# PSUM as one pool of eight banks, expert columns by single banks, and two small jobs moved to GpSimd

## The chip, the cores and the metric

One core of one Trainium2 chip runs the whole program in one launch. The metric is the device time of one execution in microseconds (us). Five engines have queues of their own, each worked through in order: TensorE (PE in the profile, PEld for its weight loads), VectorE (DVE), ScalarE (ACT), GpSimd (POOL) and SyncE (SP), which starts most transfers; GpSimd starts the indirect transfers. TensorE writes its results into PSUM, which this program uses as eight banks of 128 partitions x 512 floats.

## The reference, cut to what matters

`x` is 16 batches of 512 tokens of 128 numbers, all in 32-bit floats. Two layers follow each other:

```
xn = layernorm(x)                                # (x - mean) / sqrt(var + 1e-5)
x  = x + linear_attention(xn) + moe(xn)
xn = layernorm(x)
x  = x + chunked_softmax_attention(xn) + channel_mix(xn)
```

- Linear attention: 16 heads of 8, rotary embedding, features elu + 1, causal sums over k v; the result is divided by its causal denominator and goes through `Wo`.
- moe: 8 experts of width 512, `square(relu(x w_fc)) w_proj`; each token takes the two with the highest router probability, with weights that sum to one. A shared expert of the same form sees every token.
- Chunked softmax attention: 16 heads of 8, chunks of 64 queries that see all keys up to their chunk's end, with a gate per row from two steps of a small dynamic, and an output projection.
- Channel mix: `sigmoid(xr W_r) * (square(relu(xk W_k)) W_v)`, with xr and xk mixed from a token and the one before it.

## The kernel before, in words

**Four chains and a planner.** Batches go in five groups (3, 4, 4, 3, 2). For each group there are four generators. `dispatch` does the first layernorm, the router, the top two and the slots, and sends every token's row to its two slots in memory by 128-row indirect transfers on GpSimd (`send`, L1095). `slot_tiles` reads the slots back in tiles of 128 rows of one expert and runs the experts. `layer0` does linear attention and the shared expert, `layer1` all of the second layer, which begins with `combine`: it fetches the experts' rows (`fetch`, L1114, indirect again). The generators do not issue instructions: each call on `V`, `S`, `G`, `M` or `SP` records an operation in a `Program`, in the order in which the chains are interleaved by planned times. `Program.run` (L332) then deals out the real order. It keeps a clock for each engine with estimated costs (`COSTS`, and `TURN` for TensorE when the form of a matmul's tile changes), takes among the operations that are ready on an engine the earliest recorded (VectorE operations that read PSUM go first, `_rank`), and emits it. So the order on each engine is fixed when the program is built. All instructions so emitted have the line of the helper, L261. A `unit` is a run of matmuls that is dealt out as one piece; without it, operations of other chains can come between any two matmuls. The indirect transfers are "spaced": at least 1900 ns of the planned clock apart, and each is made to wait for the last matmul emitted before it. The square root of the layernorm is given 2600 ns more than other operations of its size.

**PSUM.** Two pools, each with its own line of requests: `ps_big`, three slots of two banks, and `ps_one`, two slots of one bank (L509). A slot that comes free goes back into a heap by its time, and the earliest free one is taken (`_take`, L414). Pairs hold scores (`sc`, `st`), the outputs by heads, q and k of both layers, the shared expert's hidden columns (`h_ps`) and the experts' (`hg_ps`); single banks hold transposes, router logits, `y` and `yg_ps`.

**Around the change.**
- `layernorm_T` (L649): mean and variance on VectorE, `ln_rstd` by a Sqrt activation on ScalarE and a reciprocal on VectorE, then `xn` on VectorE and its transposes on TensorE. It runs 32 times.
- `linear_operands` (L831): eight transposes of the features `qr` into one pair of banks (`qkT_ps`); ScalarE copies q and k out (`q0T`, `k0T`), and makes from the same PSUM tile four masked copies of q (`q0m`, two tiles of two halves), each by a Copy activation whose scale is a column of the constant `pick`. The masked copies feed the matmuls `sc<-q0m,k0T`.
- `shared_expert` (L1010) and `hidden` (L1168): two matmul groups of 512 columns fill a pair of banks, and one Relu of 128x1024 empties it; a square on VectorE or GpSimd follows. `project` (L1184) accumulates two tiles of `yg_ps` in one bank, `projected` (L1298) computes q and k of the second layer.

Of the kernel before, what the change touches and what calls it, by code (L numbers as in the profile page):

```python
# [159 lines left out]
class Base:  # L160


    def __init__(self, slots, make):
        self.slots, self.make, self.tile = slots, make, None
        self.writers, self.readers = [], []
        self.left, self.free_at, self.users = 0, 0.0, []

    def made(self):
# [5 lines left out]
class Slots:  # L174
# [1 line left out]


    def __init__(self, n, ahead):
        self.free, self.asked, self.taken, self.waiting = [0.0] * n, [], 0, []
        self.ahead = ahead  # L180


class Pool:
# [6 lines left out]
    def tile(self, shape, dtype, tag, name, bufs=None):  # L190
        n = bufs or self.bufs
        slots = self.tags.setdefault(tag, Slots(n, self.ahead))
        kw = {"bufs": bufs} if bufs else {}
        base = Base(slots, lambda: self.pool.tile(shape, dtype, tag=tag, name=name, **kw))
        slots.asked.append(base)
        base.psum = self.psum
        base.turn = len(slots.asked) - 1
        return View(base, shape)


class Op:
# [25 lines left out]
class Program:  # L227
# [21 lines left out]
    def call(self, name, api, method, args, kw):  # L249
        views = [a for a in (*args, *kw.values()) if isinstance(a, View)]  # L250
        o = kw.get("out", args[0] if args else None)
        writes = [o.base] if isinstance(o, View) else []
        reads = [v.base for v in views if v is not o]
        n = math.prod(o.shape[1:]) if isinstance(o, View) else 0
        later = 0.0

        def made(a):
            return a.made() if isinstance(a, View) else a

        def emit():  # L260
            return getattr(api, method)(*map(made, args), **{k: made(a) for k, a in kw.items()})  # L261

        if name == "PE":
            later = 60.0
            form = (args[1].shape[0], o.shape[0])
            if method == "transpose":
                cost = 112.0
            elif args[1].shape[0] == 32:
                cost = max(0.425 * n, 56.0)
            elif o.shape[0] == 32:  # L270
                cost = max(0.425 * n, 56.0)
            else:
                cost = max(1.68 * n, 224.0)
        elif method == "dma_start":
            cost, later = 80.0, 512.0 * n
        else:
            form = method if (name, method) in COSTS else None
            if name == "DVE" and method in ("tensor_scalar", "tensor_scalar_min", "tensor_scalar_max"):
                form = "fast"
            if method in ("tensor_reduce", "bn_stats"):  # L280
                n = math.prod(args[1].shape[1:])
            least, each = COSTS[name, form]
            cost = least + each * n
            if kw.get("func", args[2] if len(args) > 2 else None) == AF.Sqrt:
                cost += 2600.0
        op = self.add(name, emit, reads, writes, cost, later)
        if name == "PE":
            (self.unit_of[0] if self.unit_of else op).form = form
        return op
# [42 lines left out]
    def run(self):  # L332
# [20 lines left out]
        while emitted < len(self.ops):  # L353
# [46 lines left out]
            for base in op.bases:  # L400
                base.left -= 1
                base.free_at = max(base.free_at, end + op.later)
                if not base.left:
                    heapq.heappush(base.slots.free, base.free_at + HANDOVER)
                    waiting, base.slots.waiting = base.slots.waiting, []
                    for other in waiting:
                        offer(other, 0.0)
# [6 lines left out]
    def _take(self, op, start, offer):  # L414
# [4 lines left out]
            by_slots.setdefault(id(b.slots), []).append(b)  # L419
        ready = start  # L420
        for bs in by_slots.values():
            slots = bs[0].slots
            if len(slots.free) < len(bs):
                slots.waiting.append(op)
                return False
            if any(slots.asked[slots.taken + k] is not b for k, b in enumerate(bs)):
                ahead = bs[-1].turn - slots.taken
                if ahead > slots.ahead or not self._passes(new):
                    (slots.waiting if ahead > slots.ahead else self.put_off).append(op)
                    return False  # L430
            ready = max(ready, heapq.nsmallest(len(bs), slots.free)[-1])
        if ready > start:
            offer(op, ready)
            return False
        for bs in by_slots.values():
            slots = bs[0].slots
            for b in bs:
                heapq.heappop(slots.free)
                b.has = True
                while slots.taken < len(slots.asked) and hasattr(slots.asked[slots.taken], "has"):  # L440
                    slots.taken += 1
# [5 lines left out]
    def _passes(self, new):  # L447
# [8 lines left out]
                    also.setdefault(id(b.slots), set()).add(b)  # L456
        for bs in also.values():
            slots = next(iter(bs)).slots
            if len(slots.free) < len(bs):
                return False  # L460
            if any(b not in bs for b in slots.asked[slots.taken : slots.taken + len(bs)]):
                return False
# [26 lines left out]
def two_layers(ctx: ExitStack, tc: tile.TileContext, x, small, const, w_fc, w_proj, out):  # L489
# [16 lines left out]
    p2 = pool("p2", 2)  # L506
    p3 = pool("p3", 3)
    tiny = pool("tiny", 2)
    ps_big = pool("ps_big", 3, 24, space=bass.MemoryType.PSUM)  # L509
    ps_one = pool("ps_one", 2, 24, space=bass.MemoryType.PSUM)  # L510

    def big(name):
        return ps_big.tile([P, 2, 512], F32, tag="big", name=name)

    def one(name):
        return ps_one.tile([P, 512], F32, tag="one", name=name)

    def follows(i, first):

# [81 lines left out]
    V.reciprocal(rda, rda)  # L601
    V.tensor_mul(rda, rda, alpha)
    program.lag = 0
    eps = fixed.tile([P, 1], F32, tag="eps", name="eps")
    V.memset(eps, LN_EPS)
    zeros = fixed.tile([P, 1, D], F32, tag="zeros", name="zeros")
    G.memset(zeros, 0.0)
    program.lag = 1000
# [40 lines left out]
    def layernorm_T(xs, xT, name, tag, bufs):  # L649
# [4 lines left out]
            V.bn_stats(st[:, t, :], xs[:, t, :])  # L654
            V.bn_aggr(mv[:, t, :], st[:, t, :])
        rstd = tiny.tile([P, NT], F32, tag="ln_rstd", name=f"ln_rstd_{name}")
        S.activation(rstd, mv[:, :, 1], AF.Sqrt, bias=eps, scale=1.0)
        V.reciprocal(rstd, rstd)
        xn = p2.tile([P, NT, D], F32, tag=tag, name=f"xn_{name}", bufs=bufs)
        for t in range(NT):  # L660
            V.tensor_scalar(
# [169 lines left out]
    def linear_operands(xnT, b, home):  # L831
# [62 lines left out]
            )  # L894
        yield

        pts = big(f"qkT_ps_{b}")
        for s in range(2):
            for t in range(NT):
                M.transpose(  # L900
                    pts[:, s, t * P : (t + 1) * P], qr[:, t, s * D : (s + 1) * D], ident
                )
        q_tag, k_tag, bufs = home["T"]
        qT = p2.tile([P, T], F32, tag=q_tag, name=f"q0T_{b}", bufs=bufs)
        S.copy(qT, pts[:, 0, :])
        kT = p2.tile([P, T], F32, tag=k_tag, name=f"k0T_{b}", bufs=bufs)
        S.copy(kT, pts[:, 1, :])
        qms = []
        for u in range(2):
            tag, bufs = home["q0m"]  # L910
# [2 lines left out]
            )  # L913
            for o in range(2):
                r = 2 * u + o
                S.activation(qm[:, o, :], pts[:, 0, :], AF.Copy, scale=c_("pick")[:, r : r + 1])
            qms.append(qm)
        yield
        return qT, kT, qms
# [1 line left out]
    def linear_attention(operands, b, home):  # L921
# [4 lines left out]
        def scores(t):  # L926
# [14 lines left out]
            for pr, sc in enumerate(scs):  # L941
                tag, bufs = home["am"]
                am = p2.tile([P, 2, 512], F32, tag=tag, name=f"am_{b}_{t}_{pr}", bufs=bufs)
                V.tensor_tensor(
                    am.rearrange("p j (t q) -> p (j t) q", q=P),
                    sc.rearrange("p j (t q) -> p (j t) q", q=P),
                    causal.unsqueeze(1).to_broadcast([P, 2 * NT, P]), ALU.mult,
                )
                ams.append(am)
            return ams  # L950
# [59 lines left out]
    def shared_expert(b, xnT, oT, home):  # L1010
# [3 lines left out]
            p2.tile([P, 2, T], F32, tag="hid", name=f"h_{b}_{fp}", bufs=4) for fp in range(2)  # L1014
        ]
        for fp in range(2):
            ph = big(f"h_ps_{b}_{fp}")
            for i in range(2):
                f = 2 * fp + i
                M.matmul(  # L1020
                    ph[:, i, :], wfc_s[:, f * P : (f + 1) * P], xnT, start=True, stop=True
                )
            hf = hs[fp]
            S.activation(hf, ph, AF.Relu)
            (V if fp or b < GROUPS[0] else G).tensor_tensor(hf, hf, hf, ALU.mult)
            yield
        yield
        py = one(f"y_{b}").rearrange("p (t d) -> p t d", d=D)
        for t in range(NT):
            cols = slice(t * P, (t + 1) * P)  # L1030
            M.matmul(py[:, t, :], oT[:, cols], w_("wo0"), start=True, stop=False)
            for f in range(NF):
                M.matmul(
                    py[:, t, :], hs[f // 2][:, f % 2, cols], wpj_s[:, f, :], start=False, stop=(f == NF - 1)
                )
        V.tensor_tensor(xs, py, xs, ALU.add)
        SP.dma_start(passed["x1", b], xs.rearrange("p t d -> p (t d)"))
        yield
# [87 lines left out]
    def slot_tiles(g):  # L1126
# [39 lines left out]
            return xgT  # L1166

        def hidden(xgT, ws, q, pair):  # L1168
            ph = big(f"hg_ps_{g}_{q}_{pair}")
            for ii, (wf, _) in enumerate(ws):  # L1170
                i = 2 * pair + ii
                for f in range(NF):
                    M.matmul(
                        ph[:, ii, f * P : (f + 1) * P], wf[:, f * P : (f + 1) * P],
                        xgT[:, i * P : (i + 1) * P], start=True, stop=True,
                    )
            h = p2.tile([P, 2, FF], F32, tag="hid", name=f"hg_{g}_{q}_{pair}", bufs=4)
            o = h[:, 0 : len(ws), :]
            S.activation(o, ph[:, 0 : len(ws), :], AF.Relu)

            (V if pair or g == 0 else G).tensor_tensor(o, o, o, ALU.mult)
            return h
# [1 line left out]
        def project(h, ws, n):  # L1184

            py = one(f"yg_ps_{g}_{n}")
            for ii, (_, wp) in enumerate(ws):
                for f in range(NF):
                    M.matmul(
                        py[:, ii * P : (ii + 1) * P], h[:, ii, f * P : (f + 1) * P],  # L1190
                        wp[:, f, :], start=(f == 0), stop=(f == NF - 1),
                    )

            y = p2.tile([P, 2, D], F32, tag="yg", name=f"yg_{g}_{n}")
            m = len(ws)
# [102 lines left out]
    def projected(xT, b):  # L1298

        ps = big(f"qk1_{b}")  # L1300
        for i in range(2):
            M.matmul(ps[:, i, :], wqk1[:, i, :], xT, start=True, stop=True)
        qk = p2.tile([P, 2, T], F32, tag="qk", name=f"qk_{b}", bufs=1)
        S.copy(qk, ps)
        return qk
# [403 lines left out]
```

## Time and profile before

| | |
|---|---|
| time, median of 3 runs | 1670.35 us (1669.26 to 1676.13) |
| the profiled execution | 1665.29 us |
| its span, first to last instruction | 1663.5 us |
| mean granted clock of TensorE | 0.973 |
| instructions in the trace | 36439 |
| transfers | 167.03 MB, mean 100 GB/s |

The span lies 1.8 us inside the profiled execution's time. A group of the profile reads: line, engine, operation, output from input with shapes, how often; then busy time and mean ns of one; then the idle time of the engine just before them and who ended it. A busy time is the union of an engine's records, so a mean is that union divided by the count or the mean of single records where they overlap.

### The profile page before, as it was taken

The numbers are of one execution on the slowest core, as the hardware profiler recorded it, in microseconds if no ns is written. First come the engines' busy times: TensorE is split into PE (matmuls) and PEld (weight loads), VectorE is DVE, ScalarE is ACT, GpSimd is POOL, SyncE is SP. The second block draws the span as 40 slices with busy tenths as digits, with TensorE's granted clock in tenths as the row PEclk, the third lists the DMA queues.
The fourth block names the chain that finished last, engine by engine and source line by source line (L and its number), as shares of the span: only waits on it lengthen the run. The fifth ranks groups of instructions, "written<-read, shape, count | busy, mean of one in ns | idle before, by whom it ended". The sixth has DMA issues, their size and how long they took to land.

```text
span 1663.5 us, 36439 instructions
## 1 busy us (share of the span) xinstructions
PE 1547.3 (93%) x14439; PEld 1021.8 (61%) x14439; DVE 1207.5 (73%) x2474; ACT 778.2 (47%) x1191; POOL 539.1 (32%) x485
## 2 busy tenths in 40 slices
PE   4889799999999999999999989999999999999996
PEld 3578776666766566566666656666565656565443
DVE  7875268877578874976758796968786858786773
ACT  4343334545445634444544655454545444535444
POOL 1415255075125421453033603242136202135020
PEclk8899999999999999999999999999999999999998
DMA  5367777144334423243322243324133313110000
GB/s 155 106 211 233 219 218 212 49 141 118 96 107 127 127 87 96 72 121 97 90 90 79 78 122 96 96 63 124 35 94 92 110 33 86 30 51 23 20 1 14
DMA packets 154986, 167.03 MB, mean 100 GB/s; under 512 B 13248, under 2 KB 100672, under 8 KB 154816
## 3 DMA queue, kind: packets, MB, share of 16 engines
q1 hardware_dynamic: 146624, 147.91, 29.9%
q0 software_dynamic: 8192, 16.79, 3.3%
q8 instruction: 114, 1.87, 0.5%
q14 instruction: 56, 0.46, 0.1%
HBM read 122.83 MB, written 41.81 MB: 99 GB/s over the span
## 4 chain that ended last, share of the span: by engine, by line
PE 53%; DVE 10%; issue 5%; ACT 3%; POOL 1%; DMA 0%; SPq 0%; POOLq 0%; ACTq 0%; DVEq 0%
PE o L261 10%; PE sc L261 10%; PE st L261 8%; PE yg_ps L261 5%; PE hg_ps L261 5%; DVE maxima L261 4%; PE y L261 3%; PE h_ps L261 2%; PE qkv L261 1%; PE qk L261 1%; PE ho_a L261 1%; ACT ex L261 1%; PE oh_a L261 1%; PE mx L261 1%; PE cm_r L261 1%
## 5 line engine op out<-in xcount | busy, mean ns | idle before, releaser
L261 DVE TENSOR_REDUCE maxima<-sc 128x2 f32<-128x768 f32 (+2 forms) x448 | 385.8, 912 | 84.6 <-PE sc L261 83.0
L261 ACT ACTIVATE ex<-st 128x1024 f32<-128x1024 f32 x320 | 313.1, 1025 | 177.5 <-PE st L261 176.3
L261 PE MATMUL st<-qa,ka 32*128 32x384 f32 (+3 forms) x2048 | 213.4, 471 | 9.6 <-DVE maxima L261 5.9
L261 PE MATMUL sc<-ka,qa 32*128 32x512 f32 (+2 forms) x1792 | 213.8, 511 | 3.7 <-DVE maxima L261 1.0
L1095 POOL DMA_INDIRECT rows<-xn,pl_slot x128 | 135.1, 1055 | 225.6 <-PE y L261 64.2
L261 PE MATMUL yg_ps<-wp,hg 128*128 128x128 f32 x1304 | 188.5, 287 | 17.5 <-DVE hg L261 9.4
L261 PEld LDWEIGHTS yg_ps<-wp,hg 128*128 128x128 f32 x1304 | 162.6, 195 | 66.9 <-issue 36.6
L1114 POOL DMA_INDIRECT back<-results,pl_slot x128 | 128.4, 1003 | 222.7 <-PE st L261 38.4
L261 PE MATMUL hg_ps<-xgT,wf 128*128 128x128 f32 x1304 | 182.5, 285 | 10.8 <-issue 6.3
L261 DVE TENSOR_TENSOR am<-sc,const_sb 128x1024 f32<-128x1024 f32 x128 | 151.3, 1218 | 53.7 <-PE sc L261 49.2
L261 PEld LDWEIGHTS hg_ps<-xgT,wf 128*128 128x128 f32 x1304 | 163.5, 196 | 35.9 <-issue 23.8
L261 PE MATMUL o<-ex,vpad 128*32 128x512 f32 (+3 forms) x2048 | 175.1, 447 | 1.7 <-ACT yg L261 1.3
L261 PEld LDWEIGHTS st<-qa,ka 32*128 32x128 f32 x2048 | 104.0, 186 | 81.4 <-issue 26.4
L261 ACT ACTIVATE hg<-hg_ps 128x1024 f32<-128x1024 f32 x84 | 84.2, 1002 | 135.7 <-PE hg_ps L261 135.3
L261 POOL TENSOR_TENSOR hg<-hg 128x1024 f32<-128x1024 f32 x34 | 64.6, 1901 | 224.1 <-ACT hg L261 223.9
L261 PEld LDWEIGHTS sc<-ka,qa 32*128 32x128 f32 x1792 | 90.5, 185 | 70.5 <-issue 25.8
L261 PEld LDWEIGHTS o<-ex,vpad 128*32 128x32 f32 x2048 | 52.2, 110 | 83.8 <-issue 59.5
L261 DVE TENSOR_TENSOR hg<-hg 128x1024 f32<-128x1024 f32 (+1 forms) x50 | 62.0, 1241 | 56.4 <-ACT hg L261 56.4
L261 ACT COPY oTs<-o 128x256 f32<-128x256 f32 (+1 forms) x96 | 42.7, 445 | 120.2 <-PE o L261 119.5
L261 ACT COPY yg<-yg_ps 128x256 f32<-128x256 f32 x84 | 30.9, 368 | 131.6 <-PE yg_ps L261 108.6
L261 PE MATMUL o<-am,vpad 128*32 128x128 f32 x2048 | 81.8, 281 | 8.7 <-DVE am L261 8.0
L261 PE MATMUL sc<-q0m,k0T 32*128 32x256 f32 x1024 | 81.3, 410 | 1.6 <-ACT ex L261 1.0
(193 smaller groups left out, 2289.1 us busy)
## 6 DMA issues: line engine op xcount, KB each, us to landing
wf<-in_w_fc SPq DMA_DIRECT2D x163, 256.0 KB
wp<-in_w_proj SPq DMA_DIRECT2D x163, 256.0 KB
results<-yg SPq DMA_DIRECT2D x79, 128.0 KB
xg<-rows SPq DMA_DIRECT2D x37, 256.0 KB
rows<-zeros SPq DMA_DIRECT2D x2, 2496.0 KB
x_in<-in_x SPq DMA_DIRECT2D x16, 256.0 KB
x<-x SPq DMA_DIRECT2D x16, 256.0 KB
out<-rr SPq DMA_DIRECT2D x16, 256.0 KB
```

Source lines behind the costliest of these rows:

```text
L261: return getattr(api, method)(*map(made, args), **{k: made(a) for k, a in kw.items()})
L1095: i = nc.gpsimd.indirect_dma_start(out=rows.made()[:, :], out_offset=bass.IndirectOffsetOnAxis(ap=slot.made(), axis=0), in_=row.made(), in ...
L1114: "POOL", lambda: nc.gpsimd.indirect_dma_start(out=o.made(), out_offset=None, in_=results.made()[:, :], in_offset=bass.IndirectOffsetOnAxi ...
```

## The change

Four things change.

1. PSUM becomes one tile of eight banks. `big` and `one` ask the same line of requests (`Banks`); the planner assigns one free bank, or two adjacent free ones, and picks the placement with the least of (time it is ready + 400 ns for each bank that leaves its neighbour free). Candidates are tried by number, and a later one must be strictly better.
2. The hidden columns of both kinds of expert, and q and k transposed, take single banks; each bank is emptied by its own Relu or copy. `y`, `hg`, `yg` and `qk1` matmuls become units.
3. `q0m` is made by GpSimd from the copied `q0T` in SBUF.
4. The inverse root is made by GpSimd: add 1e-5, then raise to -0.5. The planner's extra cost for a square root goes.

The mask of the causal scores (`am`) is written with a four-dimensional pattern instead of a three-dimensional one, since the two banks are now a slice of a larger tile.

```diff
+class Banks:
+    def __init__(self, pool, n, ahead):
+        self.pool, self.n, self.whole = pool, n, None
+        self.slots = Slots(n, ahead)
+        self.slots.free = [(0.0, k) for k in range(n)]
...
+    def place(slots, bs, start):
+        free = {k: max(t, start) for t, k in slots.free}
+        best = None
+        def alone(k, rest):
+            return (k ^ 1) in rest
+        def fit(i, rest, at, ready, odd):
+            nonlocal best
+            if i == len(bs):
+                if best is None or ready + 400.0 * odd < best[0][0] + 400.0 * best[0][1]:
+                    best = ((ready, odd), list(at))
+                return
+            for k in sorted(rest):
+                ks = range(k, k + bs[i].banks)
+                if all(j in rest for j in ks):
+                    left = {j: t for j, t in rest.items() if j not in ks}
+                    cost = sum(alone(j, left) for j in ks)
+                    fit(i + 1, left, at + [tuple(ks)], max([ready] + [rest[j] for j in ks]), odd + cost)
...
-            if kw.get("func", args[2] if len(args) > 2 else None) == AF.Sqrt:
-                cost += 2600.0
...
-    ps_big = pool("ps_big", 3, 24, space=bass.MemoryType.PSUM)
-    ps_one = pool("ps_one", 2, 24, space=bass.MemoryType.PSUM)
+    banks = Banks(
+        ctx.enter_context(tc.tile_pool(name="psum", bufs=1, space=bass.MemoryType.PSUM)), 8, 48
+    )
...
-        S.activation(rstd, mv[:, :, 1], AF.Sqrt, bias=eps, scale=1.0)
-        V.reciprocal(rstd, rstd)
+        G.tensor_scalar_add(rstd, mv[:, :, 1], LN_EPS)
+        G.tensor_tensor(rstd, rstd, root, ALU.pow)
...
-        pts = big(f"qkT_ps_{b}")
-        for s in range(2):
+        q_tag, k_tag, bufs = home["T"]
+        both = []
+        for s, (tag, n) in enumerate(((q_tag, "q0T"), (k_tag, "k0T"))):
+            pts = one(f"qkT_ps_{b}_{s}")
             for t in range(NT):
...
+            oT = p2.tile([P, T], F32, tag=tag, name=f"{n}_{b}", bufs=bufs)
+            S.copy(oT, pts)
+            both.append(oT)
...
-                S.activation(qm[:, o, :], pts[:, 0, :], AF.Copy, scale=c_("pick")[:, r : r + 1])
+                G.tensor_scalar_mul(qm[:, o, :], qT, c_("pick")[:, r : r + 1])
...
-            ph = big(f"h_ps_{b}_{fp}")
...
-            S.activation(hf, ph, AF.Relu)
+                ph = one(f"h_ps_{b}_{f}")
+                M.matmul(ph, wfc_s[:, f * P : (f + 1) * P], xnT, start=True, stop=True)
+                S.activation(hf[:, i, :], ph, AF.Relu)
...
         py = one(f"y_{b}").rearrange("p (t d) -> p t d", d=D)
-        for t in range(NT):
+        with program.unit():
+            for t in range(NT):
...
         def hidden(xgT, ws, q, pair):
-            ph = big(f"hg_ps_{g}_{q}_{pair}")
...
+                ph = one(f"hg_ps_{g}_{q}_{i}")
+                with program.unit():
+                    for f in range(NF):
...
+                S.activation(h[:, ii, :], ph, AF.Relu)
...
             py = one(f"yg_ps_{g}_{n}")
+            with program.unit():
...
     def projected(xT, b):
         ps = big(f"qk1_{b}")
+        with program.unit():
```

## The prediction

> **What bounds the kernel now.** I read the page's busy line, slices and chain first, then a table of windows by stage.
>
> ```profile
> PE 1547.3 (93%) x14439; PEld 1021.8 (61%) x14439; DVE 1207.5 (73%) x2474; ACT 778.2 (47%) x1191; POOL 539.1 (32%) x485
> ...
> PE   4889799999999999999999989999999999999996
> ...
> PE 53%; DVE 10%; issue 5%; ACT 3%; POOL 1%; DMA 0%; SPq 0%; POOLq 0%; ACTq 0%; DVEq 0%
> ```
>
> ```profile
> 0.00:50.00 50.00, 25.45 (x119) 16.04 (x123) 37.23 (x145) 21.13 (x40) 10.14 (x26) 0.82 0.43 132
> 50.00:100.00 50.00, 43.80 (x534) 33.03 (x524) 40.64 (x103) 21.90 (x45) 21.86 (x22) 0.97 0.40 126
> 100.00:300.00 200.00, 180.47 (x1539) 148.31 (x1535) 125.84 (x266) 77.66 (x123) 84.22 (x72) 0.95 0.72 221
> 300.00:1600.00 1300.00, 1249.66 (x11877) 801.39 (x11880) 967.38 (x1878) 633.66 (x953) 420.23 (x364) 0.99 0.29 84
> 1600.00:1664.00 64.00, 47.89 (x394) 23.00 (x388) 36.39 (x85) 23.82 (x31) 2.66 (x3) 0.86 0.03 9
> ```
>
> The columns are length, busy time of PE, PE's loads, DVE, ACT and POOL, granted clock, DMA share, GB/s. TensorE is the bound from 100 us on (96% between 300 and 1600); only the first 50 us belong to the start and the last 64 to one batch's dependent chain. So an edit pays if it takes something out of TensorE's own queue: a matmul, a change of tile form, or a wait. ACT's 778 and POOL's 539 us are no bound by their sums.
>
> But "busy" hides short waits. I took every matmul's end, less the end before it, less its own streaming time. Streaming alone sums to 1228 us. Leaving the 128x128 form costs 197 ns (409 times), leaving a 32-row form 216 (370), leaving a 32-column form 143 (236): 194 us. The start and end are 14 us. The other 227 us of the 1663.5 are waits, by what the program makes each matmul wait for: 1273 that wait for one other engine lose 115 ns each (146 us), 186 for two 209 (39), 166 for TensorE's own earlier writes and another engine 300 (50), 58 for its own alone 88 (5); those with no wait come out at -2 ns (-12). By the engine last waited for, the gross losses are 292 us (so 0.77 of each counts): DVE 141, ACT 87, transfers 32, TensorE 27, POOL 5.
>
> Next, the groups that the edit touches, from the list of groups kept apart by shape.
>
> ```profile
> L261 ACT ACTIVATE hg<-hg_ps 128x1024 f32<-128x1024 f32 x79 | 81.2, 1027 | 128.9 <-PE hg_ps L261 128.5
> ...
> L261 ACT ACT_TABLE_LOAD x48 | 61.6, 1283 | 21.2 <-PE st L261 19.2 <-PEq L1699 0.7 <-DVE phi L261 0.6
> ...
> L261 POOL TENSOR_SCALAR ka<-qk,const_sb 128x512 f32<-128x512 f32 x32 | 50.7, 1583 | 0.0
> ...
> L261 ACT ACTIVATE q0m<-qkT_ps,const_sb 128x512 f32<-128x512 f32 x64 | 39.4, 713 | 0.0
> ...
> L261 ACT ACTIVATE ln_rstd<-ln_mv,eps 128x4 f32<-128x4 f32 x32 | 9.6, 298 | 16.4 <-DVE ln_mv L261 16.1
> ...
> L261 ACT ACTIVATE hg<-hg_ps 128x512 f32<-128x512 f32 x5 | 3.0, 599 | 6.9 <-PE hg_ps L261 6.9
> ```
>
> **Forms: -8 us.** Counted in the two programs' orders, the streaming matmuls are the same 14439, but grouping (units around y, hg, yg and qk1) cuts changes of form: 382, 348 and 250 against 409, 370 and 236. At 197, 216 and 143 ns that is 186 against 194 us. Nothing hides it.
>
> **Bank pool and single columns: -7 us (-31 to +20).** In the new program no matmul waits on TensorE's own writes (224 before), 1364 wait for one engine and 277 for two. At the old means that is 157 + 58 - 13 = 202 against 227: -25. Against it stands how soon a bank is used again. Both orders use a bank again 2430 times, but ties go to the lowest number: bank 0 gets 395 turns and bank 7 210, where the six banks of pairs had about 310 each. I measured the slack (TensorE work between the last write and the next, less the eviction's duration): 131 places below nothing against 120, 262 below 300 ns against 202, 702 below 1 us against 583. Priced by the old mean wait of each class this is 159 against 148 us: +11. Leaving out the matmuls that waited on TensorE itself it is 118 against 148 less 31 saved, which is the lower bound -31; the upper, +20, takes the shortfalls alone (65 against 47 us, 53 measured). The classes overlap with the kinds, so I take the middle of -25 and +11.
>
> **ACT: -5 us (0 to -32).** Away go 47 of 48 table loads (47 x 1.283 = 60), 32 square roots (9.6) and 64 q0m copies (64 x 0.713 = 46); each split Relu gives back 2 x 0.599 - 1.027 = 0.171, so +13 for the 79 hg pairs and +6 for the 32 h pairs. Net some -96 of 778 us, 12%. If TensorE's waits on ACT (87 x 0.77 = 67) shrank likewise: -8. But loads stand where ACT has slack:
>
> ```profile
> 732.00 1.28 ACT L261 ACT_TABLE_LOAD   x1
> 733.29 0.30 ACT L261 ACTIVATE ln_rstd<-ln_mv,eps 128x4 f32<-128x4 f32 x1
> 733.50 0.56 ACT L261 COPY oTs<-o 128x512 f32<-128x512 f32 x1
> 734.08 1.28 ACT L261 ACT_TABLE_LOAD   x1
> ```
>
> In the 228 us from 0.5 before to 3.5 after a load TensorE lost 0.181 us per us, elsewhere 0.176, so the loads cost it about 1. The far end, -32, would take away all 41 us lost in those windows. I take -5, since earlier Relu halves also release matmuls sooner. A rule that would enlarge this: the Trainium skill, "ScalarE: Activation LUTs", What ACT_TABLE_LOAD costs, adds a drain of some 1380 ns to the 1283 of the load; by it the 47 would be worth about 125 us of ACT, an estimate. The rows above leave no gap before or after the load, so here it is 1.28.
>
> **q0m on POOL: +6 us (+4 to +16).** The four halves move behind the q0T copy (0.59): ACT needed 2.4 us for its four in batch 0 (they overlap a little); POOL needs 4 x 1.58 = 6.3, by the ka row, the same operation and shape. Total 7 us, plus about 1 us for each indirect DMA interleaved (L1095, 0.96 each; up to five in batches 0, 1, 3, 4). The distance in TensorE's work from the transposes to the second q0m tile is 3.6, 6.5, 6.1, 8.3, 8.6, 9.5 us in batches 0 to 5, 6.3 to 6.9 in 6, 11 and 12, and over 14 in the rest, which hide it. The shortfalls sum to 19 us against 3 to 9 before; most of it (12) falls in batches 0 and 1, where TensorE has holes anyway. Behind a waiting q0m on POOL stand the spaced indirect DMAs of dispatch, and then the experts' gathers.
>
> **The start: +3 us (-3 to +24).** The first inverse root now needs POOL before xn, the first transposes and all that follows. Between POOL's memsets and this operation the new program puts a reload of POOL's operations. Before, the same reload stood ahead of the first hg square, inside a stretch in which POOL idled:
>
> ```profile
> 183.81 0.96 POOL L1095 DMA_INDIRECT rows<-xn,pl_slot  x1 [0.48 <-PE yg_ps L261]
> 212.71 1.89 POOL L261 TENSOR_TENSOR hg<-hg 128x1024 f32<-128x1024 f32 x1 [27.95 <-ACT hg L261]
> ```
>
> So its price lies between 0.06 (two records of 32 ns) and 28 us, less what passes under the load of x (3.8 us) and its statistics (to 5.5). I take +3, near the short records, since other work filled that stretch. A rule that speaks against the change: the Trainium skill, "GPSIMD Engine Reference", 2.1 Instruction dispatch, has the first call of freshly loaded code wait about 6 us with nothing shown in a profile. By that page the first xn would begin near 10 us, not 9, an estimate, and the start would lose about 1 to 4.
>
> **Inverse roots, later waits: +1 us (-3 to +15).** 32 pairs (add, pow) of 128x4 on POOL replace a 0.30 Sqrt and a 0.17 reciprocal. No row shows pow; bounds are 0.105 us (a memset of 128x1) and 1.9 (the 128x1024 product) each. 17 of the 32 stand right behind an indirect DMA, whose starts follow TensorE at some 1.8 us: up to 17 x 1.8 = 31 us in which xn waits, and DVE's queue (maxima, am, x) behind xn; half could reach TensorE. A gain comes where the Sqrt no longer waits behind ACT's ex. Two further instructions per group only test a semaphore on ACT and DVE (17 to 21 ns, 299 in all, already true since TensorE waited first).
>
> **Sum.** -8 - 7 - 5 + 6 + 3 + 1 = -10 us against the profiled execution's 1665.3: 1655. The runs shown have a median 5 above that execution, so on their scale 1660.
>
> **Rivals.** (1) *Waits fall further*: -31 for the banks and -14 for ACT, with q0m at +4 and nothing at the start: -8 - 31 - 14 + 4 = -49, 1621. For it: 224 self-waits vanish and half-size Relus give the first column 0.43 us earlier. Against it: DVE, which keeps its work, is behind more waits than ACT. (2) *Slower, by the dealing of banks*: the lowest free number is taken at once, so bank 0 is reused within 300 ns of slack 99 times and bank 7 thrice. Before, a freed slot came back in the order of freeing. At +20 instead of -7, the sum is +17: 1687. It decides once evictions start more than 0.3 us late, which DVE does whenever POOL's big products double its times (x<-back took 345 ns alone and 2017 beside one). (3) *Slower, by POOL's queue*: q0m +16, roots +15, else as above: +14, near 1684. (4) *A start exposed*: +24 instead of +3: +11, 1681. (5) *Nothing measurable*: the parts cancel to within 0.5%, 8 us, about what a measurement here can tell from no change. That the edit does not do what it says is excluded for counts: the built program holds one table load.
>
> **Numbers.** Forecast with its neighbours down to rival 1: faster 0.48 (rival 1 is 0.18 of it). Cancelled: 0.20. Slower 0.32: rival 2 0.14, rival 3 0.11, rival 4 0.07. For the range, the ends' distances from the sum taken as independent: upward 27, 10, 21, 14 give 38, downward 24, 27, 2, 6, 4 give 37; with rival 1 taken in, 1620 to 1698.
>
> **Right or wrong.** Right if the page shows ACT near 680 us with one table load, POOL near 650 to 700, DVE within 2% of 1207, TensorE's first matmul before 12 us and its later windows at 96 to 97%. Wrong if rows sc<-q0m wait on POOL by over 10 us after the first 100, if xn's idle names POOL by over 20, if the reused low banks show TensorE waiting for maxima, ex or am longer than the 5.9 and 1.9 us of before, or if ACT's relief turns into more than 12% less idle on TensorE.

## The result: 1690 us, 1.0% slower, and the profile after

| | before | after |
|---|---|---|
| time, median of 4 runs each | 1672.71 us (1669.26 to 1676.13) | 1690.38 us (1688.05 to 1692.35) |
| ratio | | 1.0105, 95% interval 1.0077 to 1.0133 |
| profiled execution, its span | 1665.29, 1663.5 us | 1688.05, 1686.3 us |

The forecast was 1660 us, faster; the measured time lies inside its range (1620 to 1698) but on the other side of before. First the page of the changed kernel: busy line, TensorE's slices, chain.

```profile
PE 1520.8 (90%) x14439; PEld 1006.2 (60%) x14439; DVE 1211.0 (72%) x2442; ACT 695.0 (41%) x1159; POOL 686.9 (41%) x613
...
PE   4689897899999999999998999989999999978886
...
PE 62%; DVE 18%; POOL 5%; issue 4%; ACT 3%; DMA 0%; POOLq 0%; DVEq 0%; ACTq 0%
```

ACT and POOL are where the prediction put them (near 680, 650 to 700). But POOL's share of the chain has gone from 1% to 5%, DVE's from 10% to 18%. The windows, with the columns of the prediction's table:

```profile
0.00:50.00 50.00, 26.28 (x64) 14.30 (x64) 29.36 (x120) 10.46 (x26) 13.18 (x32) 0.69 0.42 126
50.00:100.00 50.00, 35.76 (x368) 25.55 (x371) 33.15 (x87) 6.91 (x15) 36.22 (x31) 0.69 0.28 90
100.00:300.00 200.00, 174.97 (x1563) 146.85 (x1564) 115.96 (x220) 64.18 (x133) 92.63 (x83) 0.96 0.66 198
300.00:1600.00 1300.00, 1220.70 (x11899) 789.05 (x11899) 985.70 (x1921) 578.58 (x940) 533.40 (x459) 0.99 0.30 89
```

By 100 us TensorE has done 432 matmuls against 653 before, at a granted clock of 0.69 against 0.82 and 0.97. In the later windows the counts of matmuls are close (1563 and 11899 against 1539 and 11877), though TensorE is busy for 94% of 300 to 1600 us, not 96%. So against the kernel before the net loss is there at the start: the first `den` reciprocal (in the division that ends batch 0's linear attention, at 70 us before) comes 24 us later, the last one 21 us later. That is a net figure; the experiments split it into a gain and a larger loss that also grows later. Here are TensorE's first matmuls of the changed kernel, from the timeline (start, duration, tile, count, what ended the idle time before):

```profile
10.88 2.92 PE L312 MATMUL banks<-wqkv,xnT 128*128 128x384 f32 x4 [0.67 <-DVE ln_mv L312]
...
21.44 2.77 PE L312 MATMUL banks<-wqkv,xnT 128*128 128x384 f32 x4
...
32.72 2.91 PE L312 MATMUL banks<-wqkv,xnT 128*128 128x384 f32 x4
...
43.95 2.82 PE L312 MATMUL banks<-wqkv,xnT 128*128 128x384 f32 x4
...
54.42 1.24 PE L312 MATMUL banks<-const_sb,xn 128*128 128x128 f32 x4 [5.94 <-DVE xn L312]
...
66.75 1.24 PE L312 MATMUL banks<-q0m,k0T 32*128 32x256 f32 x8 [0.49 <-DVE pl_ef L312]
70.53 1.24 PE L312 MATMUL banks<-q0m,k0T 32*128 32x256 f32 x8 [2.55 <-POOL q0m L312]
```

and of the kernel before, whose qkv groups were all done by 21 us:

```profile
16.71 4.12 PE L261 MATMUL qkv<-wqkv,xnT 128*128 128x384 f32 x12
...
43.06 2.39 PE L261 MATMUL sc<-q0m,k0T 32*128 32x256 f32 x16 [0.53 <-ACT q0m L261]
```

The last groups, of what the edit touched: the work moved about as counted.

```profile
L312 POOL TENSOR_SCALAR q0m<-q0T,const_sb 128x512 f32<-128x512 f32 x64 | 101.4, 1594 | 57.9 <-ACT q0T L312 42.6 <-ACT lg L312 14.5
...
L312 POOL TENSOR_TENSOR ln_rstd<-ln_rstd,root 128x4 f32<-128x4 f32 x32 | 34.9, 1089 | 2.6
...
L312 POOL TENSOR_SCALAR ln_rstd<-ln_mv 128x4 f32<-128x4 f32 x32 | 8.6, 267 | 91.8 <-DVE ln_mv L312 90.5 <-issue 0.4
...
L312 ACT ACT_TABLE_LOAD x1 | 1.3, 1283 | 0.7 <-PEq L1767 0.7
```

### The profile page after: what moved, and what is told of

Its sections match the earlier page's. It is cut to its first block, busy times and chain, and to the rows that moved or that the text cites. A ratio compares the mean times of both kernels' runs of the same rounds, so it can differ in the third digit from the quotient of the medians.

```text
span 1686.3 us, 36720 instructions
## 1 busy us (share of the span) xinstructions
PE 1520.8 (90%) x14439; PEld 1006.2 (60%) x14439; DVE 1211.0 (72%) x2442; ACT 695.0 (41%) x1159; POOL 686.9 (41%) x613
## 4 chain that ended last, share of the span: by engine, by line
PE 62%; DVE 18%; POOL 5%; issue 4%; ACT 3%; DMA 0%; POOLq 0%; DVEq 0%; ACTq 0%
PE banks L312 62%; DVE maxima L312 6%; ACT ex L312 2%; POOL back L1179 2%; DVE am L312 1%; POOL q0m L312 1%; DVE gf_z L312 1%; DVE xn L312 1%; POOL ln_rstd L312 1%; DVE hg L312 1%; DVE gf_v L312 1%; DVE qr L312 1%; POOL ka L312 0%; DVE x L312 0%; POOL qa L312 0%
## 5 line engine op out<-in xcount | busy, mean ns | idle before, releaser
L312 DVE TENSOR_REDUCE maxima<-banks 128x2 f32<-128x768 f32 (+2 forms) x448 | 385.2, 911 | 96.8 <-PE banks L312 95.2
L312 ACT ACTIVATE ex<-banks 128x1024 f32<-128x1024 f32 x320 | 311.9, 1022 | 174.0 <-PE banks L312 156.4
L312 PE MATMUL banks<-ka,qa 32*128 32x512 f32 (+2 forms) x1792 | 194.6, 520 | 32.0 <-ACT ex L312 13.2
L312 PE MATMUL banks<-qa,ka 32*128 32x512 f32 (+3 forms) x2048 | 199.5, 465 | 16.9 <-DVE maxima L312 11.7
L312 DVE TENSOR_TENSOR am<-banks,const_sb 128x1024 f32<-128x1024 f32 x128 | 150.8, 1216 | 70.4 <-PE banks L312 63.6
L312 PE MATMUL banks<-xgT,wf 128*128 128x128 f32 x1304 | 180.6, 284 | 5.5 <-DVE maxima L312 2.0
L312 PEld LDWEIGHTS banks<-xgT,wf 128*128 128x128 f32 x1304 | 160.7, 194 | 40.9 <-issue 18.5
L312 PE MATMUL banks<-ex,vpad 128*32 128x512 f32 (+3 forms) x2048 | 177.4, 447 | 3.5 <-DVE maxima L312 2.0
L312 PE MATMUL banks<-wp,hg 128*128 128x128 f32 x1304 | 165.6, 280 | 13.8 <-DVE hg L312 5.7
L312 PEld LDWEIGHTS banks<-wp,hg 128*128 128x128 f32 x1304 | 154.4, 193 | 29.8 <-issue 12.2
L312 POOL TENSOR_SCALAR q0m<-q0T,const_sb 128x512 f32<-128x512 f32 x64 | 101.4, 1594 | 57.9 <-ACT q0T L312 42.6
```

## The experiments

All ratios are against the kernel before on the same chip, with 95% intervals. "Lag" is by how much the first and the last `den` reciprocal start later than in the profile of before (one execution each; executions of one kernel differ by up to 16 us, so a lag carries about 8).

| run | ratio | lag, first / last den |
|---|---|---|
| the change | 1.0105 (1.0077 to 1.0133) | +24 / +21 |
| e1, two lines of requests | 1.0195 (1.0169 to 1.0221) | +10 / +28 |
| e2, old PSUM, both GpSimd jobs | 1.0017 (0.9995 to 1.0040) | +17 / +19 |
| e3, PSUM part alone | 0.9917 (0.9891 to 0.9943) | +6 / -13 |
| e4, PSUM part and q0m | 1.0087 (1.0056 to 1.0118) | +17 / +25 |
| e5, PSUM part and roots | 0.9915 (0.9884 to 0.9946) | +10 / -13 |
| e6, the change, right prices | 1.0077 (1.0050 to 1.0104) | +14 / +9 |
| e7, the change, longest free bank | 1.0110 (1.0069 to 1.0150) | +21 / +21 |
| e8, before, another spacing | 0.9961 (0.9935 to 0.9987) | +2 / 0 |
| e9, e5 and spare GpSimd work | 1.0096 (1.0074 to 1.0118) | +9 / +18 |
| e10, q0m on GpSimd from batch 3 | 1.0057 (1.0038 to 1.0076) | +8 / +6 |
| e11, e5 and right prices | 0.9870 (0.9850 to 0.9890) | +5 / -31 |
| e12, old PSUM, roots | 0.9974 (0.9961 to 0.9986) | 0 / -14 |
| e13, the change, squares on ScalarE | 0.9897 (0.9876 to 0.9918) | +24 / -8 |
| e14, e11, squares on ScalarE | 0.9643 (0.9625 to 0.9661) | +9 / -52 |
| e15, old PSUM, spare work | 1.0013 (0.9990 to 1.0035) | +3 / +5 |
| e16, old PSUM, q0m | 1.0052 (1.0031 to 1.0072) | +10 / +9 |
| e17, e3 and spare work | 1.0009 (0.9989 to 1.0029) | +10 / -2 |
| e18, old PSUM, squares on ScalarE | 0.9861 (0.9825 to 0.9897) | +3 / -23 |

**First four: the parts.** My first theory was the line of requests: with one line for all banks, a pair for qkv may pass an unrelated single asked earlier only if all its users could run at once, and so the four qkv groups come one by one, as the timeline shows.

```diff
-        self.slots = Slots(n, ahead)
...
+        self.lines = {2: Line(shared, ahead), 1: Line(shared, ahead)}
...
```

`shared` holds the one list of free banks, which both lines use.

> The changed kernel, but pairs of banks and single banks have a line of requests each, over the same eight banks. Theory 1 (one line of requests makes a pair for qkv wait in the planner for unrelated singles asked earlier, so the qkv matmuls of the first two batches are dealt out one by one; the 24 us lost before 75 us come from that): the four qkv groups are done by about 25 us, the first sc matmul starts before 52 us instead of at 66.75, and the time is 1670 to 1680 against 1690. Theory 2 (the 24 us come from the GpSimd jobs, roots and masked q, standing in the start's chain): the first sc matmul stays after 60 us and the time at 1685 to 1693. Theory 3 (banks dealt by the lowest number make evictions late all along): no change, since the dealing is the same, 1686 to 1694.

Measured 1707 us, outside every range. The qkv groups were done by 24 us, as expected, and 14 us of the lag went, but the first scores came at 58.9 us, not before 52. And the time rose, with some 45 us of lag by the middle. The line of requests explains part of the order at the start, not the loss. Why two lines lose more later is open.

e2 puts the two GpSimd jobs into the kernel before, and takes the planner's extra cost for a square root out there; e3 takes both jobs out of the changed one; e4 takes the roots alone out.

```diff
 # e2, in the kernel before
-        S.activation(rstd, mv[:, :, 1], AF.Sqrt, bias=eps, scale=1.0)
-        V.reciprocal(rstd, rstd)
+        G.tensor_scalar_add(rstd, mv[:, :, 1], LN_EPS)
+        G.tensor_tensor(rstd, rstd, root, ALU.pow)
...
-                S.activation(qm[:, o, :], pts[:, 0, :], AF.Copy, scale=c_("pick")[:, r : r + 1])
+                G.tensor_scalar_mul(qm[:, o, :], qT, c_("pick")[:, r : r + 1])
...
 # e3, in the changed kernel: the roots the other way round, and
-                G.tensor_scalar_mul(qm[:, o, :], qT, c_("pick")[:, r : r + 1])
+                S.activation(qm[:, o, :], qT, AF.Copy, scale=c_("pick")[:, r : r + 1])
 # e4: the roots alone the other way round
```

> The kernel before, with the inverse root and the masked q by GpSimd and nothing else; PSUM as before. Theory 1: the start is close to that of before, up to 8 us later where masked q waits on GpSimd; time 1665 to 1682. Theory 2: most of the loss is here, first sc matmul at 60 us or later, time 1685 to 1695.

> The changed kernel, with the inverse root back as Sqrt and reciprocal and the masked q back on ScalarE (from the copied q): only the bank pool, the single columns and the units are left of the change. Theory 1: the start keeps about half or more of its loss (the fourth qkv group still comes after the routing matmul pl_both), time 1680 to 1692. Theory 2: the start is as before, first sc matmul at 43 to 48 us, and the time is 1658 to 1672, with the 224 self-waits and 8 us of form changes as a gain.

> The changed kernel with only the inverse root back as Sqrt and reciprocal, with its extra cost in the planner. Theory 1: half of the start's loss stays, first sc matmul at 52 to 60 us, time 1678 to 1688. Theory 2, roots being the larger part of the GpSimd jobs: time 1666 to 1676. If the roots cost nothing at all: 1688 to 1693.

1678.4, 1660.0 and 1690.6 us. The PSUM part is a gain of 0.8%; the roots are nothing that shows (1.0087 without, 1.0105 with them); so masked q is the loss, and e2 suggests that it is one mainly together with the new PSUM.

**Masked q by itself, prices, dealing, and an empty change.** e5 is e3's second edit alone. e6 sets prices, e7 changes the tie between banks, e8 moves a planner constant of the kernel before.

```diff
 # e6
+    ("POOL", "tensor_scalar_mul"): (120, 2.88), ("POOL", "tensor_scalar_add"): (300, 0.0),
+    ("POOL", "pow"): (1100, 0.0),
...
 # e7
-                if best is None or ready + 400.0 * odd < best[0][0] + 400.0 * best[0][1]:
+                key = (ready + 400.0 * odd, old)     # old: mean time since when its banks are free
+                if best is None or key < best[2]:
 # e8
-SPACE = 1900
+SPACE = 1950
```

> The changed kernel with only the masked q back on ScalarE (from the copied q); the inverse root stays on GpSimd. Theory A (the GpSimd jobs lose at the start by the order they give the planner, masked q about 11 us and the roots 7, worked out from the first den: +6 without either, +17 with masked q, +24 with both; and masked q loses about 20 more behind GpSimd's queue later, e4's +10 against e3's -13): the first den comes 10 to 15 us after that of the kernel before, and the time is 1655 to 1670. Theory B (the loss comes from the two jobs together filling GpSimd, neither alone matters): time below 1658. Theory C (masked q is harmless, roots are it): 1684 to 1692.

> The changed kernel with nothing but the planner's prices of three GpSimd operations set to what the profiles show: 128x512 by a column 1595 ns (planned 1016), add of 128x4 300 (127), pow of 128x4 1100 (127). Theory D (the planner, told that GpSimd's new work is short, deals out an order in which TensorE and VectorE wait for it): the start comes back, first sc matmul before 55 us, matmuls wait for masked q by under 10 us after 100 us instead of 13.6, and the time is 1660 to 1676. Theory E (GpSimd's queue is too slow and too busy for these jobs whatever the order): no more than 6 us are won, 1683 to 1692.

> The changed kernel, but between banks that are equally good the one free for longest is dealt, as the pools before did, not the lowest number. If the dealing by lowest number costs what rival 2 of the prediction says (27 us between -7 and +20): 1660 to 1675. If a bank's early reuse costs next to nothing, since the planner's clock already allows for its eviction: 1684 to 1694, the waits for evictions after 100 us (153.8 us on VectorE and ScalarE together) within 10 us.

> The kernel before with one planner constant moved a little (spacing of the indirect transfers 1950 instead of 1900 ns) and no change of the work: how far the time moves by another order alone. Theory F (the orders are about equally good, differences beyond 5 us have a cause): 1668 to 1679. Theory G (any disturbance of the order scatters the time by 10 us or more): outside 1662 to 1684.

1651.2, 1680.7, 1685.2 and 1662.2 us (before, on that chip: 1668.6). e5 settles which part it is: 1.0105 - 0.9915 = 1.9%, 32 us, are masked q on GpSimd. e5's time is below theory A's range and inside theory B's, but e4 (masked q without the roots: 1.0087) speaks against B, by which neither job matters alone. e6 met neither range: the first scores came at 45 us instead of 67, as expected, but only 0.3% was kept. Its fourth `den`, at 99 us, leads the changed kernel's by 13 us, its fifth, at 169, is 4 us behind. Prices set the order of the start, they do not give GpSimd time. e7: the dealing by lowest number costs nothing that shows. e8 came out below theory F's range, within G's limits: another order of the same work moved the time by 0.4%, so differences of that size between orders are not read as causes here.

**Chain or queue?** Masked q could cost because TensorE waits for it, or because it fills GpSimd's queue and other work comes late. e9 leaves masked q on ScalarE and gives GpSimd products that nobody reads; e10 moves masked q only from batch 3 on.

```diff
 # e9, in e5
                 S.activation(qm[:, o, :], qT, AF.Copy, scale=c_("pick")[:, r : r + 1])
+                for k in range(NT):
+                    spare = p2.tile([P, P], F32, tag="spare", name=f"spare_{b}_{r}_{k}", bufs=1)
+                    G.tensor_scalar_mul(spare, qT[:, k * P : (k + 1) * P], c_("pick")[:, r : r + 1])
 # e10, in the changed kernel
+                if b < 3:
+                    S.activation(qm[:, o, :], qT, AF.Copy, scale=c_("pick")[:, r : r + 1])
+                else:
                     G.tensor_scalar_mul(qm[:, o, :], qT, c_("pick")[:, r : r + 1])
```

> e5 (masked q on ScalarE, all else changed) plus spare work for GpSimd that nobody reads: the same products of q with the columns of pick, in 16 pieces of 128x128 per batch, written to a tile that is never read (the tile is small for want of SBUF; by the 1.58 us of 128x512 they are 6 to 10 us per batch, some 100 to 160 us in all). Theory H (GpSimd as a busy queue: indirect transfers, squares and other work come late behind masked q): most of the 32 us between e5 and the changed kernel returns, 1672 to 1690. Theory I (masked q is on a chain, what costs is that TensorE needs it and it comes late): 1648 to 1660.

> The changed kernel with masked q on ScalarE for batches 0 to 2 (the first group) and on GpSimd for batches 3 to 15. From the first den of e5 and of the changed kernel (+10 and +24 us against before) 14 us of the 32 should belong to the start and go; the other 18 should stay: 1664 to 1672. If the masked q costs only at the start: 1648 to 1658. If only later: 1676 to 1686.

1682.3 us: the spare work (256 pieces, busy for 165 us) cost 1.8%, about the 1.9 of masked q, though its 165 us are more than masked q's 101. What comes late, from the waits of TensorE and VectorE (us in total, times, longest), first e5:

```profile
PE banks L312 <- POOL xk L312: 2.5, 3, 1.2
PE banks L312 <- POOL hg L312: 0.8, 1, 0.8
...
DVE xn L312 <- POOL ln_rstd L312: 28.5, 18, 3.3
```

then e9:

```profile
PE banks L312 <- POOL hg L312: 11.1, 6, 3.4
PE banks L312 <- POOL xk L312: 6.8, 2, 5.1
...
DVE xn L312 <- POOL ln_rstd L312: 41.2, 18, 7.9
```

Squares (hg, xk) and roots, which share GpSimd's queue with the spare work, are waited for longer, and xn on VectorE with them. But the planner dealt e9 another order as well: only 10392 of the 14439 places on TensorE hold the same matmul as in e5. And in the changed kernel itself these waits are hardly longer than in e5; TensorE waits more for masked q:

```profile
PE banks L312 <- POOL q0m L312: 8.4, 5, 2.5
PE banks L312 <- POOL hg L312: 4.6, 3, 2.5
PEld banks L312 <- POOL q0m L312: 13.3, 9, 3.3
DVE xn L312 <- POOL ln_rstd L312: 27.5, 18, 3.7
```

All of TensorE's waits in these views sum to 159 us there, 142 in e5 and 164 in e9. So e9 shows that GpSimd's load can cost this much with no chain through masked q; it does not show that the 32 us came in this way.

e10 (1675.6, between its ranges) left 1.4 of the 1.9%: 8 us belong to the first group, 24 to the rest. The profiles show the second place: against e5 the changed kernel is 14 us behind at the first `den`, 12 at the sixth (191 us) and 35 at the fifteenth (676 us), e10 2 us ahead, 1 ahead and 21 behind. In that stretch the two orders differ too, and what costs there is open.

e11 combines e5 and e6; e12 is the roots of e2 alone.

> e5 with the planner's prices set right, as in e6 (pow 1100 ns, add 300, the product by a column 1595 for ka). In its order the first scores stand right after the first state, so the start's remaining +10 us should go: first sc matmul before 47 us, time 1638 to 1650. If the order of the start gains nothing on the whole: 1650 to 1660.

> The kernel before with only the inverse root by GpSimd. Theory I: masked q costs on the old PSUM too, and e2 hid it, because the roots gain there (47 table loads and 70 us of ScalarE's work go): 1648 to 1664. If e2 hid nothing and masked q costs only with the bank pool: within 6 us of e2's ratio, 1669 to 1682.

1644.1 us, the best so far, and 1662.9: on the old PSUM the roots gain 0.26% (4 us), less than e8's empty change. Masked q costs 0.4% there (e2 less e12), against 1.9% with the bank pool. With the right prices it costs as much: e6 less e11 is 2.1%, so the planner's wrong price for it is not the cause.

**Relief, and the old PSUM.** e13 and e14 let ScalarE square what GpSimd squared; e15 and e16 put the spare work and masked q alone into the kernel before; e17 puts the spare work into e3, e18 the squares into the kernel before.

```diff
 # e13, e14, e18 (hidden; shared_expert likewise)
-            (V if pair or g == 0 else G).tensor_tensor(o, o, o, ALU.mult)
+            if pair or g == 0:
+                V.tensor_tensor(o, o, o, ALU.mult)
+            else:
+                S.activation(o, o, AF.Square)
```

> The changed kernel, all its GpSimd jobs kept, with the 47 squares of 128x1024 that GpSimd makes (34 hg, 13 h, 91 us) made by ScalarE instead (about 1.0 us each). GpSimd's busy time falls from 687 to some 596 us, about that of e5 (586). Theory H (GpSimd's queue is too full): 1652 to 1674. Theory J (it is masked q and the roots themselves that come late, whatever else is queued): 1680 to 1692.

> e11 (masked q on ScalarE, prices right) with the same 47 squares on ScalarE: GpSimd down to about 495 us, less than the 539 of the kernel before. Theory H, if the queue still costs at 586 us: 1625 to 1640 against 1644. If the queue no longer costs there, or ScalarE's extra 47 us cost as much: 1640 to 1655.

> The kernel before plus the spare GpSimd work of e9 (256 products of 128x128 nobody reads, 154 us in e9). If GpSimd's load costs alike whatever the PSUM: 1690 to 1702. If it costs little with the old pools, as e2 against e12 suggests: 1668 to 1682.

> The kernel before with only the masked q by GpSimd; Sqrt stays on ScalarE. From e2 less e12: 7 us, so 1672 to 1682. If masked q costs about 30 us here too and e2 hid it by some other gain: 1692 to 1704.

> e3 (bank pool, single columns and units; roots and masked q on ScalarE) plus the spare GpSimd work of e9 that nobody reads. If e9's loss came through the inverse roots behind the spare work (and so xn on VectorE): within 0.5% of e3's ratio of 0.9917. If the bank pool's order is what does not bear a busier GpSimd, roots or not: 1.004 to 1.010, as e4 (masked q on GpSimd, no roots) at 1.0087.

> The kernel before with the 47 squares of GpSimd made by ScalarE and nothing else. If the squares themselves cost (they take 1.9 us on GpSimd and double VectorE's times beside them, x<-back 2017 ns against 345), whatever the PSUM and the queue: ratio 0.975 to 0.985, VectorE's busy time down by some 30 us. If their removal only relieved the queue that masked q and the roots had filled: 0.993 to 1.003.

1653.7, 1610.8, 1673.2, 1676.8, 1670.8 and 1645.2 us. e13 looks like relief of the queue, but e18 shows that the squares on GpSimd cost 1.4% in the kernel before, too, with nothing of the change there. So e13 proves no relief: at most the 0.7% between 2.1 and 1.4 are. e14, at 1610.8, is faster than both its ranges. The busy line of e18 says where it goes:

```profile
PE 1540.4 (94%) x14439; PEld 1021.0 (62%) x14439; DVE 1168.7 (71%) x2474; ACT 828.7 (50%) x1242; POOL 448.3 (27%) x438
```

VectorE is busy 39 us less than before with the same 2474 instructions (e13 against the change 34, e14 against e11 32; e8, with the work of before, differs from it by 7). x<-back went from a mean of 404 ns to 349, 7 of the 39 us. The Trainium skill, "SBUF — State Buffer", Who interferes with whom, says that a VectorE instruction with two SBUF inputs contends with a GpSimd instruction that reads SBUF; x<-back is of that kind, and its row agrees: its three records beside an hg product took 1.85, 1.90 and 2.31 us before, the median is 0.34. Nothing here tells this cost from that of the slower squares themselves (1.90 us on GpSimd, 1.06 on ScalarE).

What a busier GpSimd costs depends on the rest:

| added on GpSimd | old PSUM | bank pool | bank pool and roots |
|---|---|---|---|
| masked q | 0.5% (e16) | 1.7% (e4 - e3) | 1.9% (the change - e5) |
| spare work | 0.1% (e15) | 0.9% (e17 - e3) | 1.8% (e9 - e5) |

A difference of two ratios carries about 0.4% here, and another order can move the time by as much (e8). e17 (1.0009, between its two ranges) runs almost e3's order on TensorE (14003 of 14439 places hold the same matmul), and e15 mostly that of before (12922), so there the spare work acts mainly at run time and not by another order. It costs 0.9% without the roots on GpSimd and 1.8% with them; since e9's order differs from e5's, that the second half goes through the roots is not shown. Nor is it shown why the bank pool's order bears less. Contention with VectorE, as with the squares, would be another way: either kind of work goes with 4 to 11 us more of VectorE's busy time, little more than the 7 by which e8 differs from before.

The best version is e14, bank pool and single columns, roots on GpSimd, masked q and squares on ScalarE, right prices: 1610.8 us, 3.6% faster than before and 4.6% than the change (0.9643 over 1.0105).

## Why the prediction was wrong, step by step

The measured parts close: -14 us (e3, 0.83%), 0 for the roots on top of it (e5 against e3), +32 for masked q (1.90%), together +18, as measured (1690.4 - 1672.7). The forecast had -15 for forms and banks (-8 - 7), -1 for ScalarE, roots and start (-5 + 1 + 3), +6 for masked q.

- **Masked q, +6: the term that failed, by 26 us.** Its price was right (1594 ns against 1.58 us), and the waits that name it are about as small as worked out: TensorE's matmuls wait 8.4 us for q0m in five places, the longest 2.5, and its loads 13.3 in nine. The step that failed is to sum shortfalls along q0m's own chain and take that for the whole price: measured it is 32 us. The text named what stands behind q0m in GpSimd's queue and gave it no price in this term; e9 and e17 show that GpSimd's load, without the chain, can cost 1.8 and 0.9%. How the 32 us divide between queue, chain and another order is open. That 778 and 539 us of ScalarE and GpSimd "are no bound by their sums" was read as if more work there cost little: with the bank pool it cost that much at 41 to 45% busy.
- **The distances were those of the changed order, and the order was taken as given.** The loss at the start was looked for in one exposed reload. It went with the order: masked q, roots and the one line of requests each moved it (e4's +17, e5's +10, e1's +10 against +24). With it went the granted clock, which no term had: it was 0.50 from about 32 to 53 us before, from about 18 to 49 and 52 to 80 after. Two records of a 128x512 matmul of the shared expert took 1.13 us at clock 1.00 (at 25.32, before) and 1.92 at 0.50 (at 35.42, after). The Trainium skill, "TensorE: Matmul & The Clock Gate", Part 1, has a TensorE idle for some 3.4 us go to half its rate. The rows agree in part: the falls at 32 us (before) and 52 us (after) come 4 us into a gap of 9.2 and of 5.9 us, but the fall at 18 us follows no gap over 1.2 us since 11 us.
- **Banks, -7: right as a sum with the forms, doubtful inside.** By the prices of the prediction, e3's order has 186.0 us of changes of form against 194.2, as counted. But in e3's profile all waits together are, by the same sum, 228 us against 227: the -25 by kinds of wait does not show. TensorE's waits for maxima and ex went from 10.5 to 22.2 and from 5.0 to 26.0 us there. e3's gain by the runs is 14 us, by the one profile 6; the difference is within what executions vary, so the one profile does not settle it.
- **ScalarE, -5: not measured by itself.** The table loads near nothing fits: 47 loads went with the roots in e5, and e5 is level with e3; e12 gives 4 us on the old PSUM, within e8's scatter. No run shows the drain behind each load that the Trainium skill, "ScalarE: Activation LUTs", What ACT_TABLE_LOAD costs, states.
- **Rival 2, dealing by the lowest number: refuted** (e7). Its time, 1687, was met by another cause.
- **Rival 3, POOL's queue: the nearest to what was measured.** It had masked q at +16, half of the 32, and +15 for the roots, which cost nothing that shows. That the queue is how masked q loses is supported by the spare work, not shown.
- **Rival 4, the reload: refuted.** Its two records stand at 3.2 us, and the first root followed its input at once:

```profile
2.67 0.56 POOL L312 MEMSET state<- 128x256 f32 x2
5.55 0.24 POOL L312 TENSOR_SCALAR ln_rstd<-ln_mv 128x4 f32<-128x4 f32 x1 [2.32 <-DVE ln_mv L312]
5.88 1.04 POOL L312 TENSOR_TENSOR ln_rstd<-ln_rstd,root 128x4 f32<-128x4 f32 x1
```

  The first xn began at 6.95 us; in the kernel before, at 8.97. Whatever the reload took passed in the 2.3 us in which POOL waited for the statistics; the 6 us that the Trainium skill, "GPSIMD Engine Reference", 2.1 Instruction dispatch, states are not in these rows.

- **The signs.** Of the signs of being right, ScalarE (695 us, one load), GpSimd (687), VectorE (1211) and the first matmul (9.09 us) came true, the 96 to 97% of the later windows did not (94%). Of the signs of being wrong, two appeared: xn's idle names POOL for 27.5 us, and TensorE's waits for maxima and ex are 34.3 and 18.5 us, 10.5 and 5.0 before. But e5, which gained 0.85%, has 28.5 us of the first, and e3, which gained 0.83%, much of the second. These signs did not tell a loss from a gain.

Still open: why the same GpSimd work costs 0.1 to 0.5% with the old pools and 0.9 to 1.9% with the bank pool, how much of masked q's 32 us is GpSimd's queue, and where e1's later loss came from.

## What to carry to other kernels

Before work is moved to an engine that is "only" 40% busy, list what stands behind it in that engine's queue and who waits for that; then measure the load by itself with work that nobody reads. Take a bundle apart before you judge it: here a gain of 14 us, a nothing and a loss of 32 us were one change. And in an order fixed by a planner, run one empty change (e8) first: it gives a first size below which a difference needs no reason.

## What the runs showed of the hardware that was not expected

- Raising 128x4 numbers to a power took a mean of 1.09 us on GpSimd, where an add of the same size took 0.27 (the change).
- The reload of GpSimd's operations cost at most 2.3 us here, all of it hidden.
- With 47 squares of 128x1024 on GpSimd VectorE was busy for 32 to 39 us more than with them on ScalarE, with the same number of instructions (three pairs of runs, e18's the 39).
